# First convolution of a ConvNeXt-and-scan kernel: tiles of 32 rows by 64 columns of TensorE in place of one tile over 112 rows

## The chip, the cores and the metric

The kernel runs on one core of a Trainium2 chip. A time is the device time of one execution in microseconds (us). TensorE is PE in the profile, its weight loads PEld; VectorE is DVE, ScalarE ACT, GpSimd POOL, SyncE SP.

## The reference

Two layers follow one another on x of 32 images, 96 channels, 56 x 56 pixels, all in float32:

```
# layer 0
h = depthwise_conv(x, conv_w)            # 7 x 7, pad 3, each channel by itself
h = h + conv_b
h = (h - mean_c(h)) * rsqrt(var_c(h) + 1e-5) * ln_g + ln_b   # over the 96 channels
h = gelu(h @ w1 + b1) @ w2 + b2          # 96 -> 384 -> 96
x = h * layer_scale + x
# layer 1
x = silu(depthwise_conv(x, conv_w) + conv_b)   # 5 x 5, pad 2
xs = x.reshape(B, C, L)
dts, Bs, Cs = split(x_proj_w @ xs)       # 6, 4 and 4 rows
delta = softplus(dt_w @ dts + dt_b)
log_dA = max(delta * A, log 1e-9)        # 4 states for each channel
P = exp(cumsum(log_dA))
hs = P * cumsum(delta * Bs * xs / max(P, 1e-9))
y = sum_n(hs * Cs) + xs * Ds
```

This case is about the first line, the 7 x 7 convolution, and about what stands around it.

## The kernel before

The host lays x out as [96 channels, 112 rows, 896 columns]: two sets of 16 images (j = 0, 1) above one another, 56 rows each, and in a row 16 images of 56 columns. The program has four stages: the first convolution with the sums for the layer norm, the feed-forward on rows read back from memory, the second convolution, and the scan. Stages hand on through tensors in memory: conv1_d and rstd_d from the first to the second, block_d from the second to the third, conv2_d to the fourth.

**The first convolution** works a channel at a time on TensorE: a matmul sums over image rows with a banded matrix of taps, 8 times for different column shifts. It takes two image columns at once: load_x (L160) brings a channel's rows, and three copies, on POOL or DVE (L328) and on ACT (L329), sort them into xq: odd columns on partitions 0 to 55, even columns on 64 to 119. So 120 partitions are summed over, and 112 output rows come out (56 rows for each of two column parities). The four matmuls of each j (one for each t of P1 = 4, L334) read 448 columns that lie side by side in runs of 28. The banded matrices come from memory: taps1_d holds padded taps, and taps_of (L314) reads them with overlapping rows into wt.

The list of jobs sets the order: 80 channels with both j, then the last 16 channels (APART) with j = 0 and then with j = 1, so that the sums of j = 0 are complete earlier. Per job, ACT moves the result out of PSUM with the bias (L343), POOL's queue stores it in conv1_d (L347), DVE subtracts the first channel's result and adds to acc1 (L356, L357), ACT squares (L358), DVE adds to acc2 (L359). Small preparations of weights stand between the jobs (the list beside). finish_norm makes 1/sigma of the sums and stores it in rstd_d; for j = 0 it stands 14 jobs ahead of the end, for j = 1 in the feed-forward.

**The feed-forward** takes 28 groups of 4 rows. load_rows brings 1/sigma, three tiles h (32 channels by 4 rows on 128 partitions) and three tiles x for the residual (L405). normalise multiplies (L412). hidden makes 384 features from 32 channels in four row tiles (L422), ACT applies GELU (L432), result makes 32 channels in four column tiles (L441), DVE adds the bias and x (L452), twice for each result since columns are sorted by four into ot; POOL's queue stores ot in block_d (L464) with a gap between images. The order on each engine is written out by pin.

**The second convolution** reads block_d (L523) and works in four column tiles of 32 (L535); its banded taps are read from wv with a step of 8 elements. DVE and ACT sort columns (L558). The scan follows; neither is touched.

Of the kernel before, what the change touches and what calls it, by code (L numbers as in the profile page):

```python
# [8 lines left out]
F32 = mybir.dt.float32  # L9
# [14 lines left out]
WP = 128  # L24
W2 = W // 2
MP = 64
P1 = (K1 + 1) // 2
QC = 4
QW = W // QC
QR = H // 2  # L30
RW = 32
QP = QW + 1
# [6 lines left out]
EPS = 1e-9  # L39
APART = 16  # L40
# [7 lines left out]
def convnext_then_scan_kernel(  # L48
# [30 lines left out]
    conv1_d = dram.tile([C, ROWS, COLS], F32, name="conv1_d")  # L79
# [3 lines left out]
    rstd_d = dram.tile([ROWS, COLS], F32, name="rstd_d")  # L83
    taps1_d = dram.tile([C, 3 * WP * P1], F32, name="taps1_d")
# [21 lines left out]

    KR = MP + H
    PQ = HALF

# [8 lines left out]

    front = ctx.enter_context(ExitStack())
    stats = front.enter_context(tc.tile_pool(name="stats", bufs=1))  # L120
    first = stats.tile([ROWS, B2, HALF], F32, name="first")
    acc1 = stats.tile([ROWS, B2, HALF], F32, name="acc1")
    acc2 = stats.tile([ROWS, B2, HALF], F32, name="acc2")
    sq = stats.tile([ROWS, B2, HALF], F32, name="sq")

    def finish_norm(j):

        a1, a2 = acc1[:, j], acc2[:, j]
        nc.vector.tensor_mul(sq[:, j], a1, a1)
        nc.vector.scalar_tensor_tensor(  # L130
            a2, in0=sq[:, j], scalar=-1.0 / C, in1=a2, op0=ALU.mult, op1=ALU.add
        )
        nc.vector.tensor_scalar(a2, a2, 1.0 / C, 0.0, ALU.mult, ALU.max)
        nc.scalar.activation(a2, a2, AF.Sqrt, bias=eps_t[:ROWS], scale=1.0)
        nc.vector.reciprocal(a1, a2)
        for s in range(2):
            nc.gpsimd.dma_start(
                rstd_d[j * H : (j + 1) * H, s * PQ : (s + 1) * PQ], a1[s * H : (s + 1) * H]
            )

    with tc.tile_pool(name="c1", bufs=3) as pool, tc.tile_pool(
        name="c1k", bufs=1
    ) as keep, tc.tile_pool(name="prep", bufs=1) as prep, tc.tile_pool(
        name="c1_ps", bufs=4, space=PSUM
    ) as psum:
        wts = [keep.tile([128, 2, H * P1], F32, name=f"wt1_{i}") for i in range(5)]
        xqs = [keep.tile([128, B2, BI, W2 + 3], F32, name=f"xq_{i}") for i in range(3)]
        jobs = [(c, (0, B2)) for c in range(C - APART)]
        jobs += [(c, (j, j + 1)) for j in range(B2) for c in range(C - APART, C)]


        kt1 = prep.tile([C, K1, K1], F32, name="kt1")
        nc.sync.dma_start(kt1, c1w.rearrange("c (i j) -> c i j", j=K1))
        xts: dict = {}

        def load_x(n):
            c, js = jobs[n]
            xts[n] = pool.tile([128, COLS], F32, name=f"xt1_{n}", tag="xt")
            for j in range(*js):
                nc.sync.dma_start(xts[n][MP * j : MP * j + H], x[c, j * H : (j + 1) * H])  # L160

# [13 lines left out]
        c1b_t = across(c1b, ROWS, C, "c1b_t", const)  # L175
        pad = prep.tile([C, 3, WP, P1], F32, name="pad1")
        nc.vector.memset(pad, 0.0)
        at = H - 1 - K1 // 2
        for i in range(3):
            for t in range(P1):  # L180
                j = 2 * t + 1 - i
                if j in range(K1):
                    nc.vector.tensor_copy(pad[:, i, at : at + K1, t], kt1[:, :, j])
        nc.sync.dma_start(taps1_d, pad.rearrange("c d p t -> c (d p t)"))
        for t in wts + xqs + [acc1, acc2]:
            nc.vector.memset(t, 0.0)
# [119 lines left out]
        def taps_of(n):  # L306

            c, wt = jobs[n][0], wts[n % len(wts)]
            for s in range(2):
                taps = bass.AP(  # L310
                    taps1_d.tensor, taps1_d.offset + (c * 3 + 1 - s) * WP * P1,
                    [[P1, H], [WP * P1, 2], [1, H * P1]],
                )
                nc.sync.dma_start(wt[MP * s : MP * s + H], taps)  # L314

        for n in range(4):
            taps_of(n)
        for n, (c, js) in enumerate(jobs):
            if n + 4 < len(jobs):
                taps_of(n + 4)  # L320
            if n + 2 < len(jobs):
                load_x(n + 2)

            xq, xt = xqs[n % len(xqs)], xts.pop(n)
            for j in range(*js):
                xv = xt[MP * j : MP * j + H].rearrange("p (i r s) -> p s i r", i=BI, s=2)
                copy = nc.vector.tensor_copy if j else nc.gpsimd.tensor_copy
                copy(xq[:H, j, :, 2 : W2 + 2], xv[:, 1])  # L328
                nc.scalar.copy(xq[MP:KR, j, :, 1 : W2 + 1], xv[:, 0])  # L329
            wv = wts[n % len(wts)].rearrange("p o m -> p (o m)").rearrange("p (q t) -> p t q", t=P1)  # L330
            ps = bank(f"ps1_{n}")[:ROWS, :, :PQ]
            for t in range(P1):
                for j in range(*js):
                    nc.tensor.matmul(  # L334
                        ps[:, j].rearrange("p (i r) -> p i r", i=BI),
                        lhsT=wv[:KR, t],
                        rhs=xq[:KR, j, :, t : t + W2],
                        start=(t == 0),
                        stop=(t == P1 - 1),
                    )  # L340
            half = slice(*js)
            ht = pool.tile([ROWS, B2, HALF], F32, name=f"ht_{n}", tag="ht") if c else first
            nc.scalar.activation(  # L343
                ht[:, half], ps[:, half], AF.Identity, bias=c1b_t[:, c : c + 1], scale=1.0
            )
            for s in range(2):
                nc.gpsimd.dma_start(  # L347
                    conv1_d[c, js[0] * H : js[1] * H, s * PQ : (s + 1) * PQ].rearrange(
                        "(j m) q -> m j q", m=H
                    ),  # L350
                    ht[s * H : (s + 1) * H, half],
                )
            if c:

                dt = pool.tile([ROWS, B2, HALF], F32, name=f"dt_{n}", tag="dt")
                nc.vector.tensor_sub(dt[:, half], ht[:, half], first[:, half])  # L356
                nc.vector.tensor_add(acc1[:, half], acc1[:, half], dt[:, half])  # L357
                nc.scalar.activation(dt[:, half], dt[:, half], AF.Square)  # L358
                nc.vector.tensor_add(acc2[:, half], acc2[:, half], dt[:, half])  # L359
            if n >= 3 and beside:  # L360
                beside.pop(0)()
            if n == C + 1:
                finish_norm(0)
# [5 lines left out]
    with tc.tile_pool(name="mlp_ot", bufs=1) as pool_o, tc.tile_pool(  # L369
        name="mlp_g", bufs=14  # L370
    ) as pool_g, tc.tile_pool(name="mlp", bufs=2) as pool, tc.tile_pool(
        name="mlp_h", bufs=3, space=PSUM
    ) as ps_h, tc.tile_pool(name="mlp_o", bufs=2, space=PSUM) as ps_o:
        blocks = C // CB
        rts: dict = {}
        hts: dict = {}
# [4 lines left out]
            pool_o.tile([128, QC, BI, QP], F32, name=f"o_{i}") for i in range(2 * blocks)  # L381
# [4 lines left out]
        def load_rows(n):  # L386
            row = n * RB
            j, m = divmod(row, H)
            rt = pool.tile([128, COLS], F32, name=f"r_{n}", tag="r", bufs=3)
            rts[n] = rt  # L390
            for i in range(RB):
                nc.sync.dma_start(
                    rt[CB * i : CB * i + CB], rstd_d[row + i : row + i + 1].to_broadcast([CB, COLS])
                )
            for d in range(blocks):
                ht = pool.tile([128, COLS], F32, name=f"h_{n}_{d}", tag="h", bufs=9)
                for i in range(RB):
                    nc.sync.dma_start(
                        ht[CB * i : CB * i + CB], conv1_d[CB * d : CB * d + CB, row + i]
                    )  # L400
                hts[n, d] = ht
            for d in range(blocks):
                xt = pool.tile([128, COLS], F32, name=f"x_{n}_{d}", tag="x", bufs=9)
                for i in range(RB):
                    nc.sync.dma_start(  # L405
                        xt[CB * i : CB * i + CB],
                        x[CB * d : CB * d + CB, j * H + H - 1 - m - i, :],
                    )
                xts[n, d] = xt

        def normalise(n, d):
            pin(nc.vector.tensor_mul(hts[n, d], hts[n, d], rts[n]))  # L412
# [24 lines left out]
        def result(n, s, d):  # L437
# [11 lines left out]
            ot = ots[(n * blocks + d) % len(ots)]  # L449

            for e in range(2):
                pin(nc.vector.scalar_tensor_tensor(  # L452
                    ot[:, 2 * e + s, :, e : e + QW],
                    in0=po[:, :HALF].rearrange("p (i a e) -> p e i a", i=BI, e=2)[:, e],
                    scalar=b2r_t[:, d : d + 1],
# [16 lines left out]
        for d in range(blocks):  # L472
            normalise(0, d)
# [441 lines left out]
```

## Time and profile before

| | us |
|---|---|
| median of 3 runs | 3564.62 (3564.58 to 3567.93) |
| the profiled execution, its own time | 3567.29 |
| its span in the profile | 3565.5 |
| first matmul of the first convolution | 17.7 |
| first matmul of the feed-forward | 606.3 |

The page gives the busy time of each engine over the span, the span in 40 slices, the costliest groups of instructions, and the transfers. A group's row has the source line, the engine, what is written and read, partitions x elements of each, the count, then the busy time, the mean duration of one in ns, and how long the engine had stood idle ahead of these instructions and for whom. Busy time is the union of the durations, so where instructions of one engine overlap, count times mean is more than busy. The transfer table says that the first convolution's image loads are 192 of 196 KB, its tap loads 224 of 98 KB, its stores mostly 158 of 196 KB.

### The profile page before, as it was taken

To read this page: it belongs to the slowest core of one execution; us is meant where nothing else is said; L and a number is where in the kernel's file an instruction comes from. 1 tells how busy PE (TensorE), PEld (TensorE's weight loads), DVE (VectorE), ACT (ScalarE), POOL (GpSimd) and SP (SyncE) were. 2 spreads that over 40 slices of the span, in tenths; PEclk is the share of its full clock that TensorE was granted. 3 is DMA by queue.
4 is the path that set the end of the run, shared out by engine and by line. 5 is a ranking of instruction groups with operands and counts; after the bars stand their busy time and mean duration, and the time that the engine had idled before them with its cause. 6 is when DMAs were issued, how large, how long until landed. Compare 5 with 4: busy or idle time off the path is not lost. (4 is left out here: it accounts for less than half of the span.)

```text
span 3565.5 us, 47085 instructions
## 1 busy us (share of the span) xinstructions
PE 3047.3 (85%) x17290; PEld 1291.7 (36%) x17290; DVE 2664.8 (75%) x1820; ACT 2351.5 (66%) x2168; POOL 1969.4 (55%) x1284
## 2 busy tenths in 40 slices
PE   8999999999999999799857777777777777777785
PEld 5777776333333333334322222222222222222221
DVE  6666667333333333799959999999999999999998
ACT  4555555334334333688778888888888887888885
POOL 2333343222222222000059999999899999999996
PEclk9999999999999999999956766666666666667666
DMA  6655556555555552899888787787778787887873
GB/s 185 194 178 167 173 168 197 159 159 162 162 161 164 164 159 67 244 280 290 273 257 278 264 281 261 268 279 256 264 263 270 267 272 250 290 259 260 287 255 120
DMA packets 316654, 793.97 MB, mean 223 GB/s; under 512 B 133560, under 2 KB 195024, under 8 KB 291880
## 3 DMA queue, kind: packets, MB, share of 16 engines
q1 hardware_dynamic: 269888, 671.99, 59.6%
q0 software_dynamic: 29632, 80.27, 7.0%
q10 hardware_dynamic: 16904, 38.70, 2.8%
q8 instruction: 137, 2.24, 0.3%
q14 instruction: 93, 0.76, 0.1%
HBM read 555.05 MB, written 235.74 MB: 222 GB/s over the span
## 5 line engine op out<-in xcount | busy, mean ns | idle before, releaser
L713 POOL TENSOR_TENSOR rep<-rep,bt 128x1568 f32<-128x1568 f32 x192 | 674.3, 3512 | 377.7 <-DMA rep<-du_d 377.7
L742 POOL TENSOR_TENSOR hs<-hs,ct 128x1568 f32<-128x1568 f32 x191 | 669.3, 3504 | 101.3 <-DVE hs L730 89.6
L723 DVE TENSOR_TENSOR_SCAN pv<-rep,pv 128x1568 f32<-128x1568 f32 x192 | 664.5, 3461 | 42.9 <-ACT rep L709 26.2
L432 ACT ACTIVATE g<-ph,b1p_t 128x896 f32<-128x896 f32 x336 | 320.0, 1003 | 489.7 <-PE ph L422 489.7
L452 DVE SCALAR_TENSOR_TENSOR o<-po,b2r_t,x 128x224 f32<-128x224 f32 x336 | 191.0, 611 | 545.5 <-PE po L441 534.7
L334 PE MATMUL ps<-xq,wt 120*112 120x448 f32 x1536 | 582.5, 540 | 17.7 <-DMA wt<-taps_d 17.7
L464 POOL DMA_DIRECT2D block_d<-o x336 | 183.1, 552 | 637.1 <-DVE o L452 603.9
L334 PEld LDWEIGHTS ps<-xq,wt 120*112 120x112 f32 x1536 | 429.3, 280 | 169.1 <-issue 20.2
L422 PE MATMUL ph<-h,w1r_t 32*128 32x448 f32 x4032 | 430.2, 555 | 6.9 <-DVE h L412 4.8
L641 PE MATMUL pz<-xs,wd_t 96*96 96x392 f32 x512 | 282.1, 718 | 164.6 <-ACT du L649 121.6
L441 PE MATMUL po<-g,w_t 128*32 128x448 f32 x4032 | 413.1, 543 | 0.0
L760 PE MATMUL py<-hs,sel_t 128*32 128x392 f32 x1536 | 323.1, 676 | 60.5 <-POOL hs L742 60.5
L688 PE MATMUL pk<-bn,pick_t 8*128 8x392 f32 x1024 | 291.7, 692 | 95.0 <-ACT y L769 83.1
L726 DVE SCALAR_TENSOR_TENSOR pv<-pv,rep 128x1568 f32<-128x1568 f32 x192 | 345.6, 1800 | 21.6 <-POOL rep L713 1.7
L730 DVE TENSOR_TENSOR_SCAN hs<-rep,carry_h,pv 128x1568 f32<-128x1568 f32 x96 | 334.1, 3480 | 10.0
L535 PE MATMUL ps<-xq,wt 128*32 128x448 f32 x3072 | 308.6, 549 | 37.5 <-DMA xq<-block_d 35.5
L558 DVE COPY st<-yt 28x896 f32<-28x896 f32 x288 | 318.0, 1104 | 27.8 <-ACT yt L549 17.5
L730 DVE TENSOR_TENSOR_SCAN hs<-rep,pv 128x1568 f32<-128x1568 f32 x96 | 328.4, 3421 | 9.6
L708 ACT ACTIVATE rep<-rep,lift_t 128x1568 f32<-128x1568 f32 x192 | 307.6, 1602 | 6.3
L709 ACT ACTIVATE rep<-rep,lift_t 128x1568 f32<-128x1568 f32 x192 | 307.6, 1602 | 6.3
L752 PE MATMUL py<-xs,dsm_t 96*96 96x392 f32 x512 | 300.7, 728 | 10.5 <-ACT bn L676 4.7
L707 ACT ACTIVATE rep<-rep,a_t 128x1568 f32<-128x1568 f32 x192 | 308.3, 1606 | 1.7 <-DMA rep<-du_d 1.3
(90 smaller groups left out, 3136.8 us busy)
## 6 DMA issues: line engine op xcount, KB each, us to landing
rep<-du_d SPq DMA_DIRECT2D x191, 1568.0 KB
du_d<-du SPq DMA_DIRECT2D x126, 588.0 KB
xq<-block_d SPq DMA_DIRECT2D x192, 225.0 KB
block_d<-o POOLq DMA_DIRECT2D x336, 120.0 KB, 3.1
xt<-in_x_dram SPq DMA_DIRECT2D x192, 196.0 KB
x<-in_x_dram SPq DMA_DIRECT2D x336, 112.0 KB
h<-conv_d SPq DMA_DIRECT2D x336, 112.0 KB
conv_d<-st SPq DMA_DIRECT2D x96, 392.0 KB
```

Source lines behind the costliest of these rows:

```text
L334: nc.tensor.matmul(ps[:, j].rearrange("p (i r) -> p i r", i=BI), lhsT=wv[:KR, t], rhs=xq[:KR, j, :, t : t + W2], start=(t == 0), stop=(t = ...
L422: pin(nc.tensor.matmul(phs[i // 2][:, i % 2, :HALF], lhsT=w1r_t[rows, d, f * 128 : (f + 1) * 128], rhs=hts[n, d][rows, s * HALF : (s + 1) ...
L432: nc.scalar.activation(gt, ph[:, :, :HALF], AF.Gelu, bias=b1p_t[:, f : f + 1], scale=1.0)
L441: pin(nc.tensor.matmul(po[CB * i : CB * i + CB, :HALF], lhsT=w2_t[:, f, CB * d : CB * d + CB], rhs=gts[n, s, f, i // 2][:, i % 2], start=( ...
L535: pin(nc.tensor.matmul(ps[RW * f : RW * f + RW, h, : B * QW].rearrange("p (b q) -> p b q", q=QW), lhsT=wv[:, f, t], rhs=xv[:, :, t : t + Q ...
L558: pin(copy(st[:, :, :, :, f], yt[RW * f : RW * f + QR].rearrange("p h (b q) -> p h b q", q=QW),))
L713: pin(nc.gpsimd.tensor_mul(ut, ut, bts[i // NG]))
L723: pin(nc.vector.tensor_tensor_scan(grown, da, zero, pv[:, last : last + 1] if q else 1.0 / EPS, ALU.mult, ALU.add))
L726: pin(nc.vector.scalar_tensor_tensor(run, in0=grown, scalar=1.0, in1=ut, op0=ALU.min, op1=ALU.mult))
L730: pin(nc.vector.tensor_tensor_scan(ht, da, run, carry_h[:, col : col + 1] if q else 0.0, ALU.mult, ALU.add))
L742: pin(nc.gpsimd.tensor_mul(ht, ht, cts[k]))
L760: pin(nc.tensor.matmul(py[g * DG : (g + 1) * DG, s, :BK], lhsT=sel_t, rhs=hss[k * NG + g][:, cols], start=False, stop=True, tile_position= ...
```

## The change

The first convolution takes TensorE in tiles of 32 rows by 64 columns. A job is four blocks of 32 image rows, one for each row tile: two channels by two halves of the 56 rows, or, for the last 16 channels, four channels by one half. Each block brings the 28 rows that it gives and 4 more of the other half. A matmul sums over 32 image rows and gives 28 rows for a pair of neighbouring output columns (56 of 64 columns used); the two pairs of four columns are the two column tiles. Both sets of images lie in one row of 1792 columns, and the matmul reads every fourth column of it directly from the loaded tile; where the shift would leave the image, it covers 13 of 14 columns. So the copies into xq are gone. There are 8 taps j, two pairs p and four row tiles k: 64 matmuls of 448 or 416 columns for a job, in 48 jobs.

What else goes with it: conv1_d and rstd_d are laid out by halves h and pairs p. The stores of conv1_d stand on ACT's queue, two for a job. The sums run over 128 partitions and 1792 columns. load_rows and its tiles move ahead of the first convolution's pools, and the first two groups' rows are loaded and normalised within the last jobs. The feed-forward's groups go by halves of the image, 4 rows and a pair p; the residual x is loaded for two groups at once, from a pool of its own that opens when the convolution's pools close. The sum with the residual is one operation for each result instead of two, ot is [4, 32 images x 15] with five buffers for six, and each store of block_d writes one row of 7680 bytes for each channel. On SP's queue a job's four tap loads and four image loads stand three jobs ahead of its matmuls.

```diff
-        jobs = [(c, (0, B2)) for c in range(C - APART)]
-        jobs += [(c, (j, j + 1)) for j in range(B2) for c in range(C - APART, C)]
+        jobs = [[(c, 0), (c, 1), (c + 1, 0), (c + 1, 1)] for c in range(0, C - APART, 2)]
+        whole = len(jobs)
+        jobs += [
+            [(c + k, h) for k in range(JT)] for h in range(2) for c in range(C - APART, C, JT)
+        ]
...
         def load_x(n):
-            c, js = jobs[n]
-            xts[n] = pool.tile([128, COLS], F32, name=f"xt1_{n}", tag="xt")
-            for j in range(*js):
-                nc.sync.dma_start(xts[n][MP * j : MP * j + H], x[c, j * H : (j + 1) * H])
+            xts[n] = pool.tile([128, 2 * COLS], F32, name=f"xt1_{n}", tag="xt")
+            for k, (c, h) in enumerate(jobs[n]):
+                nc.sync.dma_start(
+                    two(xts[n][RW * k : RW * k + RW]),
+                    x[c].rearrange("(j m) q -> m j q", m=H)[h * (H - RW) : h * (H - RW) + RW],
+                )
...
-            for j in range(*js):
-                xv = xt[MP * j : MP * j + H].rearrange("p (i r s) -> p s i r", i=BI, s=2)
-                copy = nc.vector.tensor_copy if j else nc.gpsimd.tensor_copy
-                copy(xq[:H, j, :, 2 : W2 + 2], xv[:, 1])
-                nc.scalar.copy(xq[MP:KR, j, :, 1 : W2 + 1], xv[:, 0])
...
-            for t in range(P1):
-                for j in range(*js):
-                    nc.tensor.matmul(
-                        ps[:, j].rearrange("p (i r) -> p i r", i=BI),
-                        lhsT=wv[:KR, t],
-                        rhs=xq[:KR, j, :, t : t + W2],
-                        start=(t == 0),
-                        stop=(t == P1 - 1),
-                    )
+        def convolve(n):
+            wv = wts.pop(n).rearrange("p (o j) -> p j o", j=PJ)
+            xv = xts.pop(n).rearrange("p (b q f) -> p f b q", q=QW, f=QC)
+            pss = [bank(f"ps1_{n}_{a}") for a in range(JT // 2)]
+
+            order = sorted(range(PJ), key=lambda j: j != K1 // 2)
+            for j in order:
+                for p in range(2):
+
+                    far, g = divmod(2 * p + j - K1 // 2, QC)
+                    lo, hi = max(0, -far), QW - max(0, far)
+                    for k in range(JT):
+                        rows = slice(RW * k, RW * k + RW)
+                        nc.tensor.matmul(
+                            pss[k // 2][MP * p : MP * p + MP, k % 2, :HALF].rearrange(
+                                "p (b q) -> p b q", q=QW
+                            )[:, :, lo:hi],
+                            lhsT=wv[rows, j],
+                            rhs=xv[rows, g, :, lo + far : hi + far],
+                            start=(j == order[0]),
+                            stop=(j == order[-1]),
+                            tile_position=(RW * k, MP * p),
+                        )
+            return pss
...
+            for p in range(2):
+                if n < whole:
+                    to = conv1_d[c : c + 2, :, p].rearrange("a h m (f q) -> (m f) (a h) q", f=2)
...
+                nc.scalar.dma_start(to, hs[MP * p : MP * p + 2 * QR])
...
+            for ks, a1, _ in parts:
+                nc.vector.tensor_add(a1, a1, flat(dt[:, ks]))
+            nc.scalar.activation(dt, dt, AF.Square)
+            for ks, _, a2 in parts:
+                nc.vector.tensor_add(a2, a2, flat(dt[:, ks]))
...
+        for n in range(len(jobs)):
+            if n + 3 < len(jobs):
+                load_taps(n + 3)
+                load_x(n + 3)
+            pss = convolve(n)
+            if n == whole + len(jobs[whole:]) // 2:
+                finish_norm(0)
+            hs = evict(n, pss)
+            if n == 0:
+                first = hs
+            add_sums(n, hs)
...
+            if n == len(jobs) - 3:
+                load_rows(0)
+                load_rows(1)
+            if n == len(jobs) - 2:
+                for d in range(blocks):
+                    normalise(0, d)
...
-            for e in range(2):
-                pin(nc.vector.scalar_tensor_tensor(
-                    ot[:, 2 * e + s, :, e : e + QW],
...
+            pin(nc.vector.scalar_tensor_tensor(
+                ot[:, f].rearrange("p (b r) -> p b r", r=QP)[:, :, at : at + QW],
```

## The prediction

> **What bounds the kernel now.** I read the page's busy shares, then the busy time by stage, then the groups.
>
> ```profile
> span 3565.5 us, 47085 instructions
> PE   8999999999999999799857777777777777777785
> 0.00:601.00 601.00, 583.29 (x1546) 430.57 (x1546) 382.43 (x515) 310.47 (x416) 197.17 (x332) 1.00 0.61 182
> 601.00:1425.00 824.00, 817.09 (x8030) 305.26 (x8032) 279.82 (x425) 323.61 (x341) 184.25 (x335) 1.00 0.51 150
> 1425.00:1800.00 375.00, 320.64 (x3136) 136.89 (x3128) 328.13 (x304) 277.31 (x198) 6.52 (x12) 0.95 0.89 264
> 1800.00:3565.50 1765.50, 1326.24 (x4584) 418.97 (x4584) 1674.43 (x578) 1440.07 (x1214) 1581.49 (x606) 0.67 0.78 261
> ```
>
> The four rows of busy time (stretch and its length, then PE, weight loads, DVE, ACT, POOL, granted clock, DMA share, GB/s) are the four stages: first convolution, feed-forward, second convolution, scan. In the first, PE is busy 583.3 of 601 us at clock 1.00, DVE 382, DMA 0.61. It starts at 17.7 us and then hardly stops, so PE alone sets this stage. The feed-forward is bound by PE too (817 of 824), the last two by DVE and the transfers. The change rewrites the first stage; the others keep their arithmetic.
>
> ```profile
> L334 PE MATMUL ps<-xq,wt 120*112 120x448 f32 x1536 | 582.5, 540 | 17.7 <-DMA wt<-taps_d 17.7
> L334 PEld LDWEIGHTS ps<-xq,wt 120*112 120x112 f32 x1536 | 429.3, 280 | 169.1 <-issue 20.2 <-ACT xq L329 0.4
> L422 PEld LDWEIGHTS ph<-h,w1r_t 32*128 32x128 f32 x4032 | 192.2, 185 | 246.6 <-issue 158.0 <-ACT g L432 84.3 <-DMA h<-conv_d 3.2
> L535 PEld LDWEIGHTS ps<-xq,wt 128*32 128x32 f32 x3072 | 133.2, 141 | 213.0 <-issue 194.6 <-ACT st L558 12.1 <-DMA xq<-block_d 4.1
> L441 PEld LDWEIGHTS po<-g,w_t 128*32 128x32 f32 x4032 | 114.1, 109 | 274.2 <-issue 223.4 <-DVE h L412 50.8
> ```
>
> A matmul of the program leaves two records: 768 of them make the 1536 of L334. Between 200 and 500 us 267 records start per 100 us, 374.5 ns each, for 448 columns: 0.836 ns a column. The mean of 540 ns is not the price, since matmuls overlap.
>
> Two things must be read from other stages. First, **how tiles run together**:
>
> ```profile
> 900.28 0.13 PEld L441 LDWEIGHTS po<-g,w_t 128*32 128x32 f32 x4 [0.24 <-issue]
> 900.66 0.13 PEld L441 LDWEIGHTS po<-g,w_t 128*32 128x32 f32 x4 [0.25 <-issue]
> 902.76 0.20 PEld L422 LDWEIGHTS ph<-h,w1r_t 32*128 32x128 f32 x4 [0.17 <-issue]
> 903.13 0.20 PEld L422 LDWEIGHTS ph<-h,w1r_t 32*128 32x128 f32 x4 [0.17 <-issue]
> ```
>
> In this order of time (start, length), four column tiles (L441) load within 0.13 us and the next four 0.38 us later; four row tiles (L422) the same. So four tiles of 448 columns take the time of one. Eight tiles at once do not occur.
>
> Second, **what a stride costs**. L441 loads 32 weights that lie side by side in 109 ns. L535 loads 32 weights 32 bytes apart, 141 ns in the mean and 136 at full clock: 0.84 ns more for each. L334 loads 112 weights 16 bytes apart in 280 ns, against 185 ns for 128 side by side (L422). A strided weight costs about 1.67 ns, a contiguous one 0.8. ACT shows it too: its copies with an 8-byte step (L329) take 607 ns for 448, those with a 16-byte step (L558) 2040 ns for 896, twice as much per element.
>
> [...]
>
> **The change part by part.**
>
> *PE.* 48 jobs of 8 taps x 2 column pairs x 4 row tiles: 3072 matmuls, 6144 records, half of 448 and half of 416 columns, mean 432. Both operands now step: weights by 32 bytes, the image by 16 (every fourth column of the row). [...]If it pays what weights pay, a record takes 432 x (0.836+0.84) = 724 ns, if not 361. Eight at once: a job has 128 records, 16 rounds. So 11.6 us or 5.8 us a job; 48 jobs are 556 or 277 us. Before: 1536 x 0.3745 = 575 us. I take the strided price, since it is the same engine reading the same memory: **-19 us**. A load of 64 strided weights (about 110 + 32 x 1.67 = 163 ns) hides in 724.
>
> *Copies removed.* ACT loses 116.6 us (L329), POOL 59.4, DVE 39.6 (L328). All lay beside PE: nothing.
>
> *Eviction, sums, stores.* The same elements: per job two evictions of 1.01 us (the half jobs four of 0.62), three DVE operations of 1792 columns (1.09 us for 896 and 0.64 for 448, so 1.99), a Square of 1.70. On ACT's queue the order is eviction, two stores (about 0.45 each from ACT's other issues), Square, next eviction. Square waits for two DVE operations, so the ring is 2.0 + 2 x 1.99 + 1.70 = 7.7, with hand-overs 8.0 us. It hides under 11.6, not under 5.8. The stores leave POOL's queue, which was not waited for.
>
> *Transfers.* A job moves 917 KB of image (32 rows for 28), 262 KB of taps and 803 KB out: 2.0 MB in 11.6 us is 171 GB/s, against 182 now. SP issues 8 transfers a job at about 0.37 us. The load of h_0 stands in SP's queue behind xt_19 and waits for job 15's store; three jobs are loaded ahead, so nothing.
>
> *Start.* Eight image loads (1.83 MB) now go ahead of the tap store, where four (0.80 MB) did. At 185 GB/s that is at most 5.6 us; the smaller pad and fewer copies give some back. 0 to +6, I take **+3**.
>
> *Feed-forward.* Same matmuls in the same order. The 336 sums of 0.61 us become 168 of twice the columns, below PE anyway. The x loads of the first groups no longer run during the convolution: they wait for the last sums' buffers, some 10 us after the last matmul, and land about 5 later, while the first use is two parts of 14.5 us in. Cover is about 7 us; if it fails the stage slips by up to 10. With the last block_d writes twice as large (12 x 246 KB where 123 KB), which the second convolution waits for, I take 0 to +10, **+1**.
>
> *Sum.* -19 + 3 + 1 = -15 and, since before lost 8.6 us inside its stage (583.8 from first to last matmul against 575) where the new order has deeper loads, up to another -8: I take -20 in all. Against the profiled execution's 3567.3 us this is 3547; it lies 2.7 us (0.08%) above the median of 3564.6, so against the median **3545**.
>
> **Rivals.**
>
> *A. The image's stride is free.* [...]Against: weights come at the same pace and do pay. Then PE needs 5.8 us a job and ACT's ring of 8.0 binds: 48 x 8.0 = 384, about 6 more for the half jobs, start 21, end 411 for 601: -190, so **3375**. Transfers would be at 247 GB/s, which the second convolution exceeds. [...]a tighter ring 3330.
>
> *B. Eight tiles do not run together at the strided rate (slower).* The place is the pair of column tiles that read the same 32 partitions at different columns[...]. For: nothing shows two strided image streams from one partition. Against: L535's four loads step 32 bytes through the same partitions at once, 136 ns each. It decides from 724 x (1 + 20/556) = 750 ns a round on. If the loads alone come out from under cover, 724 + 163 = 887 ns, 681 us: +125 against the 556, so about **3670**. If the pair takes turns, 1112 us: **4100**.
>
> *C. A late transfer.* The feed-forward's x loads or the tap start cost all of their bounds: -20 turns to about 0, **3565**. Against: the covers above.
>
> That the copies would stay is excluded: in the built order PE reads xt itself and no copy of it is left.
>
> **How the numbers follow.** Main case with C at its edge 0.57 (3525 to 3575 by itself: 0.43 below 3557, 0.08 within, 0.06 above); A 0.20; B 0.23, half of it below 3700. A measurement of this kernel can tell 0.2%, 7 us, from no change. Faster 0.63, same 0.08, slower 0.29. The range takes in A's 3375 with some room, the main case and B's cheaper end: 3360 to 3700 leaves out 0.07 below and 0.11 above.
>
> **What would show it.** Right: records of the new matmul line start eight per 0.70 to 0.75 us, PE is busy through the stage, the last matmul ends near 580 us. A: rounds of 0.36 us, PE idle a quarter of the stage with waits on ACT's eviction. B: rounds over 0.75 us, or four tiles a round. The forecast is wrong on its own ground if DVE or DMA, not PE, is dense in this stage, or if the feed-forward's 824 us moved by more than 10.

## The result and the profile after

The changed kernel takes **3590.93 us** in the median (3587.80 to 3593.45, 4 runs), the kernel before 3566.27 us beside it on the same chip: a ratio of **1.0071 [1.0059, 1.0084]**. It is slower by some 25 us, under 1% but clear of the interval, where 20 us less were forecast.

The head of the page of the changed kernel, with PE's busy tenths over 40 slices of the span:

```profile
span 3589.0 us, 53661 instructions
PE   7999999999999999899948777777777777777775
```

The span grew by 23.5 us (3565.5 before). Now the busy time by stage of the changed kernel; the columns are the stretch, its length, then PE, weight loads, DVE, ACT, POOL (number of instructions), granted clock, DMA share, GB/s:

```profile
0.00:650.00 650.00, 619.12 (x6294) 535.65 (x6298) 329.76 (x249) 190.81 (x176) 13.49 (x21) 0.99 0.61 165
650.00:1475.00 825.00, 813.87 (x8032) 302.67 (x8028) 256.29 (x258) 318.08 (x333) 81.16 (x168) 0.99 0.51 153
200.00:300.00 100.00, 100.00 (x1041) 82.47 (x1033) 48.61 (x24) 28.82 (x24) 0.00 (x0) 1.00 0.58 165
```

The third row is the middle of the first convolution: PE 100 of 100 us at full clock, DVE 49, ACT 29, POOL nothing (the copies are gone), DMA 0.58. PE alone sets the stage, as before. In these 100 us 1033 records start (the row's x1041 also counts those that were still running at 200 us): 129 rounds, one per 0.774 us. A round here is one record on each of the eight tiles. The groups of the new line:

```profile
L360 PE MATMUL ps<-xt,wt 32*64 32x448 f32 (+1 forms) x6144 | 598.7, 949 | 22.9 <-DMA wt<-taps_d 22.9
L360 PEld LDWEIGHTS ps<-xt,wt 32*64 32x64 f32 x6144 | 526.3, 194 | 91.0 <-issue 45.4
```

PE is busy 598.7 us on this line where L334 was 582.5, after a first wait of 22.9 us where it was 17.7. By the starts of the records, a round of eight takes 796 ns for 448 columns and 750 ns for 416, **773** in the mean. A job comes every 12.403 us, 775 ns for each of its 16 rounds; the forecast had 724.

The span's 23.5 us, split at the same events in both traces:

| stretch | before | after | difference | forecast |
|---|---|---|---|---|
| to the first matmul | 17.7 | 22.9 | +5.2 | +3 |
| first to last matmul of the convolution | 583.8 | 600.3 | +16.5 | -24 |
| to the feed-forward's first matmul | 4.8 | 2.3 | -2.5 | in the next |
| feed-forward, to its last result | 822.5 | 826.7 | +4.2 | +1 |
| sum | | | +23.4 | -20 |

The feed-forward's last result is the end of its last matmul. The second convolution and the scan shift with it. Of the 43 us between forecast and result, 40 lie in the second row: what a round costs.

### The profile page after: what moved, and what is told of

Read it like the earlier page. It is cut to its first block, busy times and chain, and to the rows that moved or that the text cites. A ratio compares the mean times of both kernels' runs of the same rounds, so it can differ in the third digit from the quotient of the medians.

```text
span 3589.0 us, 53661 instructions
## 1 busy us (share of the span) xinstructions
PE 3052.1 (85%) x21898; PEld 1382.0 (39%) x21898; DVE 2577.2 (72%) x1371; ACT 2219.1 (62%) x1915; POOL 1676.4 (47%) x795
## 5 line engine op out<-in xcount | busy, mean ns | idle before, releaser
L496 ACT ACTIVATE g<-ph,b1p_t 128x896 f32<-128x896 f32 x336 | 319.9, 1003 | 487.6 <-PE ph L486 487.6
L360 PE MATMUL ps<-xt,wt 32*64 32x448 f32 (+1 forms) x6144 | 598.7, 949 | 22.9 <-DMA wt<-taps_d 22.9
L518 DVE SCALAR_TENSOR_TENSOR o<-po,b2r_t,x 128x448 f32<-128x448 f32 x168 | 171.5, 1021 | 561.5 <-PE po L505 551.3
L360 PEld LDWEIGHTS ps<-xt,wt 32*64 32x64 f32 x6144 | 526.3, 194 | 91.0 <-issue 45.4
L529 POOL DMA_DIRECT2D block_d<-o x168 | 81.2, 490 | 731.1 <-DVE o L518 669.5
L705 PE MATMUL pz<-xs,wd_t 96*96 96x392 f32 x512 | 271.2, 693 | 177.8 <-ACT du L713 127.6
```

The costliest lines, as they stand in the source:

```text
L360: nc.tensor.matmul(pss[k // 2][MP * p : MP * p + MP, k % 2, :HALF].rearrange("p (b q) -> p b q", q=QW)[:, :, lo:hi], lhsT=wv[rows, j], rhs ...
L496: nc.scalar.activation(gt, ph[:, :, :HALF], AF.Gelu, bias=b1p_t[:, f : f + 1], scale=1.0)
```

## The experiments

Three reasons for the dear round were possible: the 16-byte step of the image, the pair of column tiles that read the same partitions, and the weights' step of 32 bytes. Each of the first four kernels below, made from the changed kernel, removes or isolates one.

### The image without its step (e1_sorted)

The host lays a row's columns out sorted by four, so that the columns of one matmul lie side by side. Tiles, order and instruction counts stay; loads come in runs of 7168 bytes (their edits and that of the residual are left out below).

```diff
-            xv = xts.pop(n).rearrange("p (b q f) -> p f b q", q=QW, f=QC)
+            xv = xts.pop(n).rearrange("p (f b q) -> p f b q", q=QW, f=QC)
...
-        "x": v["x"].reshape(B2, BI, C, H, W).transpose(2, 0, 3, 1, 4).reshape(C, ROWS, COLS),
+        "x": v["x"].reshape(B, C, H, QW, QC).transpose(1, 2, 4, 0, 3).reshape(C, H, 2 * COLS),
```

> The changed kernel with one thing undone: the host lays each image row out with its columns sorted by four, so every matmul of the first convolution reads its image side by side (weights still 32 bytes apart); the residual is read side by side too, and loads have one run of 7168 bytes for each row. Theory S (the 16-byte step doubles what an image column costs): a round of eight tiles falls from 775 ns to 361 plus whatever of the 51 ns excess is not the image's, so 365 to 415; PE needs 5.8 to 6.6 us a job, the ring of ACT (eviction, Square behind two DVE sums) of about 8.0 to 8.4 us binds instead, the stage ends near 415 us and the time is 3375 to 3400. Rival T (eight tiles are limited by something else, such as issue or the pair of tiles on one row group): rounds stay near 775 and the time near 3590.

Measured: **3392.74 us**, ratio **0.9519 [0.9505, 0.9533]**. The group, the middle of the stage, and PE's, ACT's and DVE's longest waits between 100 and 300 us (total, times, longest):

```profile
L360 PE MATMUL ps<-xt,wt 32*64 32x448 f32 (+1 forms) x6144 | 340.5, 542 | 66.3 <-ACT hs L382 28.3
```

```profile
200.00:300.00 100.00, 91.11 (x1662) 73.89 (x1650) 76.62 (x39) 44.69 (x39) 0.00 (x0) 1.00 0.91 254
```

```profile
ACT dt L420 <- DVE acc L419: 111.7, 26, 4.6
DVE acc L422 <- ACT dt L420: 45.9, 26, 1.8
PEld ps L360 <- ACT hs L382: 40.8, 44, 1.3
```

A round is now 376 ns for 448 columns and 350 for 416: 0.839 ns a column, the price of a column in the kernel before, where records start every 376.9 ns (0.841 a column). With the step it was 796 / 448 = 1.777 ns. So the step doubles the round, **+0.94 ns a column**, and eight tiles do run together. The loads have longer runs too, but e5_step8 below keeps them as they were and takes nearly the same time, so they are not the reason. PE busy falls to 340.5 us and PE is no longer the bound: it waits for ACT's eviction (L382), ACT's Square (L420) for DVE, DVE for the Square. That ring of waits takes 7.78 us a job; the forecast's rival A had worked it out as 8.0, and 3375 us for the kernel. From first to last matmul the stage lasts 387 us. The hand-over to the feed-forward's first matmul grows to 17 us (2.3 in the changed kernel), in which PE waits for normalised rows from DVE, and the feed-forward takes 830 us (826.7).

### The weights without their step (e2_weights)

The matmul takes 64 weights that lie side by side in the same tile, thus other weights than the convolution's.

```diff
-            wv = wts.pop(n).rearrange("p (o j) -> p j o", j=PJ)
+            wv = wts.pop(n).rearrange("p (j o) -> p j o", j=PJ)
```

> The changed kernel, but each tile takes 64 weights that lie side by side in the same loaded tile (other weights than the convolution's, same loads, same image reads). Theory W (the strided weight loads take memory accesses from the strided image reads of the same partitions, which is the 51 ns by which a round exceeds 724): weight loads take about 135 ns instead of 194, a round 724 to 740, the stage 27 to 39 us less, time 3550 to 3565. Rival E (a fixed cost of eight tiles, or the pair of image reads): round unchanged at 775, time 3590 within 5.

Measured: 3589.59 us, ratio 1.0071 [1.0054, 1.0088]. The group of its weight loads and the middle of the stage:

```profile
L360 PEld LDWEIGHTS ps<-xt,wt 32*64 32x64 f32 x6144 | 411.8, 149 | 200.9 <-issue 157.5 <-DMA wt<-taps_d 0.5 <-DVE wd_t L307 0.2
```

```profile
200.00:300.00 100.00, 100.00 (x1047) 71.81 (x1039) 48.99 (x25) 29.70 (x25) 0.00 (x0) 1.00 0.59 166
```

A load shrinks from 194 to 149 ns and the rounds stay at 790 and 750 ns (796 and 750), far from the 724 to 740 of the theory that the weights' step makes the excess. The loads lie under the matmuls; their step is not the loss.

### Four tiles at a time (e3_four)

The pair p becomes the outer loop, so that four row tiles of one column half come in turn and the two column tiles no longer alternate in the program.

```diff
-            for j in order:
-                for p in range(2):
+            for p in range(2):
+                for j in order:
```

> The changed kernel with the two column pairs as the outer loop and the taps inside: only the four row tiles of one pair are in flight at a time, two groups of four one after another where eight ran together. If two strided image reads from one partition do run side by side (the theory), four tiles alone take 724 to 775 ns a round too, twice as many rounds: stage about 1110 to 1190 us, time 4100 to 4180. If that round is 724 and not 775, the excess belongs to the pair. Rival (the memory is already saturated by the pair, so eight tiles gain nothing): a round of four takes about 390 and the time stays at 3590.

Measured: 3905.25 us in one run. The records of the line (min/median/max of the duration, first and last start), and the middle of the stage:

```profile
L360 PE MATMUL ps<-xt,wt x6144: 917/962/1059, 22.1 to 936.4; 32*64 32x448 f32 x100, 32*64 32x416 f32 x99
```

```profile
200.00:300.00 100.00, 100.00 (x673) 36.05 (x670) 30.63 (x16) 19.41 (x17) 0.00 (x0) 0.98 0.36 101
```

Inside a pair, four records start every 790 ns (448 columns) or 745 ns (416): half the tiles in the time of eight. So the second column tile costs next to nothing, and the price sits in each strided record by itself. This rules out the pair as the cause. The total came out 200 us below what was expected, since for about a third of each job (6.4 of 18.8 us) eight records again start per 0.75 us. They stand around the change of pair. The trace does not name the tile of a record, but its shape tells enough. In the program, around the change within a job, each row tile has six records of 448 columns, two of 416 (the last tap of the first pair), two of 448 (the first tap of the second), two of 416 and six of 448. By their starts in the trace they are eight of 448, four of 416 and six of 448, in 47 of the 48 jobs. So the second pair's first matmuls start ahead of the first pair's last one and run beside it.

### The image with a step of 8 bytes (e5_step8)

The matmul reads every second column instead of every fourth, so the step is 8 bytes. It takes other columns than the convolution's.

```diff
-            xv = xts.pop(n).rearrange("p (b q f) -> p f b q", q=QW, f=QC)
+            xv = xts.pop(n).rearrange("p (b q f) -> p f b q", q=2 * QW, f=2)
...
-                            rhs=xv[rows, g, :, lo + far : hi + far],
+                            rhs=xv[rows, g % 2, :, lo + far : hi + far],
```

> The changed kernel, but the matmuls read image columns 8 bytes apart in place of 16 (other columns than the convolution's, same loads, same number). Theory L[...]: rounds as if side by side, 365 to 415 ns, ACT's ring binds, time 3375 to 3405. Rival P (the cost grows with the step): rounds in between, 500 to 600, time 3430 to 3490, or unchanged at 775 if any step costs.

Measured: 3399.47 us in one run. The middle of its stage:

```profile
200.00:300.00 100.00, 99.91 (x1648) 72.68 (x1640) 77.75 (x39) 44.31 (x39) 0.00 (x0) 1.00 0.94 256
```

The rounds take 403 ns (448 columns) and 407 ns (416), 27 and 57 ns more than side by side, and a job comes every 7.78 us as in e1_sorted. So a step of 8 bytes costs little, and one of 16 bytes adds 420 ns to the round of 448 columns. No run steps the image by 12 or by 32 bytes, so the runs put the jump between 8 and 16 bytes; what makes it is not shown.

### The same step in the kernel before (e9_before16)

Does the price belong to the tiles at all? The kernel before keeps its single tile of 120 rows by 112 columns, its order and its values, but the sorted columns in xq lie four elements apart, where the copies write them and the matmul reads them.

```diff
-        xqs = [keep.tile([128, B2, BI, W2 + 3], F32, name=f"xq_{i}") for i in range(3)]
+        xqs = [keep.tile([128, B2, BI, W2 + 3, 4], F32, name=f"xq_{i}") for i in range(3)]
...
-                        rhs=xq[:KR, j, :, t : t + W2],
+                        rhs=xq[:KR, j, :, t : t + W2, 0],
```

> The kernel before with one edit: the sorted columns in xq lie four elements apart, so the copies write, and the matmul of 120 rows by 112 columns reads, with a step of 16 bytes; values and order unchanged. If a column with a 16-byte step costs 1.78 ns whatever the tiling (as eight tiles of 32 rows by 64 columns and four tiles showed), a record takes about 0.79 us for 0.3745, the stage 1536 x 0.79 = 1213 us for 575, the time 4190 to 4215. If the part above the price of a strided weight (0.94 against 0.84 ns) belongs to the row tiles: 0.75 us, time 4130 to 4150. If only row tiles pay the step: within 20 us of 3565.

Measured: **4205.76 us** in one run, 640 us above the kernel before. Its matmul and copies, and the middle of the stage:

```profile
L334 PE MATMUL ps<-xq,wt 120*112 120x448 f32 x1536 | 1211.8, 967 | 17.8 <-DMA wt<-taps_d 17.7
L329 ACT COPY xq<-xt 56x448 f32<-56x448 f32 x192 | 190.6, 993 | 544.7 <-PE ps L334 534.5
L328 POOL COPY xq<-xt 56x448 f32<-56x448 f32 x96 | 94.1, 980 | 745.2 <-issue 710.1
```

```profile
200.00:300.00 100.00, 100.00 (x128) 35.65 (x127) 29.89 (x32) 31.47 (x32) 17.43 (x24) 1.00 0.26 79
```

127 records start in these 100 us where it was 265, 788 ns apart in the median where it was 376.9 in the mean: +0.92 ns for each of 448 columns. The copies with a 16-byte step are slower too (607 to 993 ns on ACT) and stay hidden. So the single tile pays the same price, and the kernel before did not pay it only because its copies had put the columns side by side.

### What binds next (e4_ring)

e1_sorted left ACT and DVE waiting for one another. Here, in e1_sorted, a job's sums come after the next job's eviction, in an order on ACT that is written out (the pin edits are left out below), so that ACT has something to do while DVE subtracts.

```diff
-            if n == whole + len(jobs[whole:]) // 2:
-                finish_norm(0)
             hs = evict(n, pss)
             if n == 0:
                 first = hs
-            add_sums(n, hs)
+            else:
+                add_sums(n - 1, last)
+            last = hs
+            if n == whole + len(jobs[whole:]) // 2:
+                finish_norm(0)
...
+        add_sums(n, last)
```

> The kernel with the columns sorted by the host (e1_sorted: 3392.7 us, a job each 7.78 us), and the sums of a job moved behind the eviction of the next job: on ScalarE's queue the order is eviction of job n+1, its two stores, Square of job n. Theory: the chain eviction, subtraction, Square of ScalarE and VectorE set the 7.78 us; apart, VectorE needs 3 x 2.03 = 6.1 us a job, TensorE 5.8, and 1.98 MB a job at the 285 to 290 GB/s which this kernel's busiest stretches reach 6.9 us, so a job each 6.5 to 7.0 us, 38 to 60 us less in all, time 3335 to 3358. Rival: the transfers (DMA share 0.91 in that stage) already bind at 7.78 us: 3380 to 3393.

Measured: **3363.40 us** (3358.04 to 3369.61), ratio **0.9434 [0.9417, 0.9452]**. The middle of the stage:

```profile
200.00:300.00 100.00, 97.13 (x1819) 81.97 (x1813) 85.94 (x43) 48.91 (x42) 0.00 (x0) 1.00 0.97 287
```

The ring was the bound: the median job takes 6.83 us, inside the 6.5 to 7.0 that was expected, and DMA share is 0.97 at 287 GB/s. At that rate the 1.98 MB of a job take 6.9 us, so by this reading the transfers bind now; no run moves fewer bytes to test it. The time stayed 5 us above the expected range, since the first five jobs still take 6 to 11 us each: over all 48, matmul to matmul, the mean is 7.43 us (8.06 in e1_sorted).

### The late start (e8_start)

e4_ring with the first eight image loads behind the store of the padded taps on SP's queue.

```diff
-        for n in range(2):
-            load_x(n)
...
         nc.sync.dma_start(taps1_d, pad.rearrange("c p f j -> c (p f j)"))
+        for n in range(2):
+            load_x(n)
```

> e4_ring with the first two jobs' eight image loads placed behind the store of the padded taps on SyncE's queue, so that this store and the loads of the banded taps that wait for it do not share the transfers with 1.83 MB of image. Theory: that order made the first matmul late (22.9 us in the changed kernel, 17.7 before); now 16 to 18 us, and 3 to 5 us less than e4_ring. Rival: the image is then what comes last, or a later transfer takes the gain back: the first matmul at 20 us or later, or the time within 1 us of e4_ring.

Measured: 3361.84 us (3356.70 to 3366.70), ratio 0.9426 [0.9412, 0.9440]. The wait ahead of its first matmul (total, times, longest):

```profile
PE ps L359 <- DMA wt<-taps_d: 19.7, 1, 19.7
```

The tap store goes out at 7.2 us instead of 14.9 and the first tap load at 14.5 instead of 19.7, but the first matmul comes only 2.1 us earlier, at 19.7 us and short of the 16 to 18 that were expected: the first tap loads now take 5.2 us from issue to use where it was 2.1. The eight image loads now stand right ahead of them on SP's queue; whether that is the reason is not shown. The kernel before, with the same 14.5, started at 17.7. The time differs from e4_ring's by 1.6 us, less than the runs spread. The order explains a part of the start's +5.2; that it is worth anything in the end is not shown.

## Why the prediction was wrong, step by step

**The bound** was read rightly: PE set the stage before and sets it after, at clock 1.00, with DVE and ACT below half and DMA at 0.58.

**Eight tiles together** held. That was the author's estimate from the four of the trace of before (groups of four loads 0.38 us apart); 376 ns a round in e1_sorted, against 376.9 for one record of the kernel before, shows that eight cost the time of one, and with the step the rounds of four (e3_four, 790 ns) and of eight (796 ns) are nearly equal.

**"An image column pays what weights pay" is the step that failed**, in size and not in kind. That the image pays for its step held: a column with a 16-byte step costs about twice (1.777 against 0.839 ns). But the price of +0.84 ns was the author's estimate from loads of 32 weights, and the image pays +0.94 (e1_sorted) or +0.92 (e9_before16). The round became 773 ns for 724, and 16 rounds in 48 jobs make 594 us for 556: +38, against a gain that was put at 19. Why a column costs a tenth more than those weights stays open.

Could the forecast have known? Weight loads do not give one price. The 64 weights of the changed kernel lose 194 - 149 = 45 ns by their step, 0.7 ns each (e2_weights), the 32 of L535 0.84. And the forecast's own lines held a nearer one: from L535's 32 weights (136 ns) to L334's 112 (280 ns, with the image's own step of 16 bytes), each further strided weight costs 144 / 80 = 1.80 ns, not the 1.67 that was taken for all. Seen afterwards, that makes an estimate of 432 x 1.80 = 778 ns a round, and 773 came. Since the three readings differ, none of them was safe to borrow. The forecast's working put the point of no gain at 750 ns, 3.6% above its 724, and its main case gave 0.06 to a slower kernel. With a borrowed price this uncertain, that chance should have been several times as large, by size alone and without a new mechanism. A rival "the image's price is a tenth higher" was missing.

**What before lost inside its stage** was misread. The forecast's 267 records per 100 us are a count that takes in those running across the edges of the stretch. By their starts, 796 records stand between 200 and 500 us, one per 376.9 ns. So the 1536 records make 579 us and not 575, and the stage of 583.8 us loses 5 us and not 8.6. At the forecast's own price the tiles would thus have gained 23 us instead of 19, and the further 5 that it counted had nothing to come from: the new stage loses 600.3 - 594 = 6 of its own. The two errors nearly cancel.

**Two smaller slips** changed nothing. The load of 64 strided weights was put at 110 + 32 x 1.67 = 163 ns, but 110 ns is the load of 32 weights without a step. From the 136 ns with one it is 190, and 194 was measured, which stays hidden under the matmuls. And ACT's copies with a 16-byte step cost 2040 / 896 = 2.28 ns an element against 607 / 448 = 1.35, so 1.7 times as much and not twice.

**Copies, eviction, sums, stores** were rightly costed at nothing. The copies were four for a whole job and two for a half one, all beside PE, and in the middle of the new stage ACT is busy 29% of the time and DVE 49%.

**The start** cost +5.2 for +3, inside its bounds of 0 to 6.

**The feed-forward** with the hand-over to it cost 4.2 - 2.5 = +1.7 for +1, inside its bounds, but not for the reason given. PE's first matmuls of that stage, three lines of the kernel before and four of the changed one (start, length, idle before and releaser):

```profile
606.30 4.97 PE L422 MATMUL ph<-h,w1r_t 32*128 32x448 f32 x28 [4.78 <-DVE h L412]
613.02 6.64 PE L422 MATMUL ph<-h,w1r_t 32*128 32x448 f32 x48 [1.75 <-ACT g L432]
620.03 2.52 PE L422 MATMUL ph<-h,w1r_t 32*128 32x448 f32 x20 [0.38 <-ACT g L432]
625.45 4.86 PE L486 MATMUL ph<-h,w1r_t 32*128 32x448 f32 x28 [2.24 <-ACT hs L382]
633.81 4.86 PE L486 MATMUL ph<-h,w1r_t 32*128 32x448 f32 x24 [3.50 <-ACT g L496]
640.54 2.54 PE L486 MATMUL ph<-h,w1r_t 32*128 32x448 f32 x24 [1.86 <-ACT g L496]
643.45 2.52 PE L486 MATMUL ph<-h,w1r_t 32*128 32x448 f32 x20 [0.38 <-ACT g L496]
```

PE stood idle for 6.9 us here before and for 8.0 after, now each time for ACT, which has the last job to finish:

```profile
623.19 2.21 ACT L382 ACTIVATE hs<-ps,c1b_t 128x448 f32<-128x448 f32 x4 [4.16 <-PE ps L360]
625.43 0.79 ACTq L395 DMA_DIRECT2D conv_d<-hs  x2
629.74 1.70 ACT L420 ACTIVATE dt<-dt 128x1792 f32<-128x1792 f32 x1 [4.34 <-DVE acc L419]
631.46 1.28 ACT L496 ACT_TABLE_LOAD   x1
632.75 1.91 ACT L496 ACTIVATE g<-ph,b1p_t 128x896 f32<-128x896 f32 x2
634.67 1.28 ACT L133 ACT_TABLE_LOAD   x1
637.50 0.67 ACT L133 ACTIVATE acc<-acc,eps_t 128x448 f32<-128x448 f32 x1 [1.54 <-DVE acc L132]
638.18 1.28 ACT L496 ACT_TABLE_LOAD   x1
```

The last job's eviction, stores and Square stand on ACT's queue ahead of the first GELU (L496), and the Square waits for DVE's subtraction and sum: ACT does nothing for 4.34 us but issue the stores. This Square covers 1792 columns (1.70 us) where that of a half job of before had 448 (0.58 us). Then the square root of finish_norm (L133) stands between the GELUs, with a load of a function table of 1.28 us on either side; in the kernel before it came ahead of the first GELU, with one such load between them. The forecast looked at the transfers of x here; DVE did wait 7.4 us for x (L518), but PE did not wait for DVE. No run moves the Square or the square root, so their shares are read from the trace alone.

**Rival A** (the step is free) fell; its 3375 us is what e1_sorted nearly shows once the step is gone. **Rival B** (the pair can't run together) fell by e3_four, although its sign, rounds above 750 ns, came. **Rival C** (a late transfer eats the gain) doesn't account for it: start, hand-over and feed-forward together miss by 3 us.

So where did the expected gain go? A job holds two channels, for which the kernel before needed 32 records one after another; the changed kernel needs 128, in 16 rounds of eight. With columns side by side a round costs what one record cost (376 against 377 ns), and the stage falls from 584 us to 387 (e1_sorted): the tiles are worth 197 us. Reading every fourth column in place of the copies costs 213 us (387 to 600) and spends all of it. The copies that the change removed lay beside PE and cost nothing; what they did, putting columns side by side, was worth more than the tiles.

## What to carry to other kernels

For a matmul in float32, look at the innermost step of the moving operand (the image here) before its tiling: a step of 16 bytes doubled its time in both tilings tried (376 to 796 ns for 448 columns in eight tiles, 377 to 788 in one), and a step of 8 bytes cost about a tenth (403 ns for 448 columns, 407 against 350 for 416). A copy (as in the kernel before) or a host layout (as in e1_sorted) that removes the step is worth having while it lies off the critical path. Where a forecast's sign hangs on a price taken from another kind of instruction, work out at which price it turns, and give the other side the chance that the borrowed price's error deserves.

## What the runs showed of the hardware that was not expected

- Four and eight tiles of 32 rows by 64 columns take the same time per round with a 16-byte step (790 and 796 ns for 448 columns): two strided streams out of the same partitions cost 6 ns a round more than one.
- The step's price hardly depends on the tile: +0.94 ns a column for 32 x 64, +0.92 for 120 x 112.
- A strided weight has no single price. A step of 32 bytes costs 0.70 ns each for 64 weights (149 to 194 ns, e2_weights) and 0.84 for 32 (109 to 136 ns, two lines of the kernel before); why they differ is open.
- Matmuls on different column tiles did not always start in program order. In e3_four the second pair's first matmuls start ahead of the first pair's last one in 47 of the 48 jobs, by the shapes and starts of the records (around the change eight of 448 columns, four of 416 and six of 448, where the program has six, two, two, two and six for a row tile).
